# Fifty-two products of a constant tile with itself on TensorE's queue, from the launch to slot 4, in a two-layer cross-attention kernel

## The chip, the cores and the metric

The kernel runs on one core of one Trainium2 chip. A core has five engines with a queue each: TensorE (PE in the profile; its weight loads stand apart as PEld), VectorE (DVE), ScalarE (ACT), GpSimd (POOL) and SyncE (SP). The last of them, and in places ScalarE, issue DMA transfers. The metric is the device time of the whole program in microseconds (us), as the median of several executions.

## The reference

Two cross-attention layers follow each other on x of shape (16, 256, 320), with one context of shape (16, 256, 512) and 20 heads of 16. Of the context's 256 tokens, layer 0 takes the first 77 as text and the other 179 as image tokens; layer 1 takes the first 252 as text and the last 4 as image tokens. Layer 0, cut to what is computed:

```python
q = hidden_states @ Wq
k_text, v_text = text @ Wk, text @ Wv
probs = softmax(einsum('bhqd,bhkd->bhqk', q_h, k_h) * scale)
text_out = einsum('bhqk,bhkd->bhqd', probs, v_h)
scores = einsum('bhqd,bhkd->bhqk', q_h, ip_k_h) * scale
text_probs = softmax(einsum('bqc,bkc->bqk', q, k_text) * scale)
sem = einsum('bqc,bnc->bqn', einsum('bqk,bkc->bqc', text_probs, text), ip) * scale
ip_probs = softmax(scores + 0.5 * sem[:, None]) * spatial_mask[None, None, :, None]
out = (text_out + einsum('bhqk,bhkd->bhqd', ip_probs, ip_v_h)) @ Wout + bout + residual
```

Layer 1 has the same form, with a normalized semantic term for each head, and takes the output of layer 0 as its x. The products that the change adds belong to none of this: nothing reads them.

## The kernel before

**Slots.** Each layer is cut into NS = 80 slots; a slot is one of the 16 batch elements and four of its heads (five slots to an element). The loop at the end of the kernel runs the slots of layer 0 with `slot0(k)` and those of layer 1 with `slot1(k)`. What isn't the inner attention (projections of queries, keys and values, the semantic term, weights, the output projection) is cut into small steps, kept as `task` entries with due times in slots; `fill(now)` issues the steps that are due. So a step due at 1.85 comes late in slot 1. `RAMP` squeezes the due times of the first slots.

**A slot of layer 0.** `maxima0` turns the row maxima of the next slot's scores with two products against an identity (L752), copies them to `mt`, and four DMAs lay them as extra rows into `qs`. `score0` (L744) makes the scores of the slot after next in PSUM tile S for half of the queries at a time, and VectorE reduces them to maxima (L745, L746). `turned0` (L768) makes the scores of this slot turned over, in the two T tiles; ScalarE takes their exponential (L771) and GpSimd multiplies it with the semantic factor (L774). `attend0` multiplies the previous slot's probabilities with the values (L801, 24 instructions) into the one P tile, and `settle0` has VectorE read this tile: a transpose (L812), a reciprocal whose result is written back into the tile's first 16 columns (L815), a product there with the spatial mask (L816), and the product that reads these columns last (L818). `stacks` issues the DMAs that fill `qs` and `ks` for the slot LEAD = 4 ahead.

**PSUM tiles.** `kept` holds a ring of whole tiles for each of the tags T (two tiles) and P (one tile); `own(tag)` hands them out in turn. So `kept["P"][1]` is the one P tile that `attend0` and `settle0` use, and `kept["T"][1]` the first of the two T tiles.

**The beginning.** `begin()` is written out by hand: loads (`land`), the rounding of each operand into a high and a low part (`high` on ScalarE, `low` on VectorE or GpSimd), and the first keys, queries, semantic terms and values, up to the scores and maxima of slots 0 and 1. In it the order of all engines is the order of the code. In the loop only TensorE's order is that of the code; the orders of the other engines are planned from modelled times when the kernel is built, with some of them tied by `queued` and `anchor`. Tiles carry their dependencies: whoever writes a tile waits for those who still read that part of it.

**Number formats.** Most products are in fp32r (one instruction each). Products of plain F32 operands, as L801, L1064 and L468, take two instructions each, as the counts of the profile show (L468 is one product and stands there with two instructions).

Of the kernel before, what the change touches and what calls it, by code (L numbers as in the profile page):

```python
# [43 lines left out]
def RAMP(t):  # L44
    return t if t < -5 or t > 3 else (t + 5) * 0.375
PINNED = {getattr(mybir.EngineType, e) for e in ("PE",)}
BANKS = {"T": 2, "P": 1, "X": 3}


@with_exitstack  # L50
def xattn2(
# [27 lines left out]
    nc = tc.nc  # L79
    f = lambda ap: ap.bitcast(F32)  # L80
# [19 lines left out]
    def own(tag):  # L100

        n, *ring = kept[tag]
        kept[tag][0] += 1
        return ring[n % len(ring)]

    def scores(kept=False):

# [227 lines left out]
    def fields():  # L335

        ind0 = buf("nt", [128, 2, 8, 32], bufs=2, name="ind0").rearrange("p a f c -> p (a f c)")[:3, :S]
        dma(ind0[:2], ind0_d)
        dma(ind0[2:], ind0_d[:1])
        yield  # L340
        ind0r = buf("mt", [8, S], FR, name="ind0r")[:3]
        nc.scalar.copy(ind0r, ind0)
        yield
        for i in range(SIZES["NR"]):
            dma(ks[i][XROW + T0 : KS0, :, :T0], ind0r[:2, :T0].unsqueeze(1).to_broadcast([2, 4, T0]))
        for i in range(2):
            dma(buf("M", [TR, 2, S], FR, bufs=SIZES["M"])[T0:, 0], ind0r)
            dma(buf("tph", [TR, 2, S], FR, bufs=2)[T0:, 0], ind0r)
        yield
# [166 lines left out]
    def weights4(l):  # L516
        wo.append((yield from weights((wo0_d, wo1_d)[l], "wF", tmask[:, 4:5], (0.1, 0.3)[l], "rawc")))
# [186 lines left out]
    def stacks0(k, parts="KQTM"):  # L704
        b, g = divmod(k, NG)
        Q, K = QK[k] = qs[k % SIZES["NR"]], ks[k % SIZES["NR"]]
        for part in parts:
            if part == "K":
                anchor(dma(K[0:XROW], stack_rows(kd[0][b // 2][:, :, b % 2], g)))
            elif part == "Q":  # L710
                dma(Q[0:XROW], stack_rows(get("q0", b)[1], g))
            elif g < SIZES["NR"]:
                tph, mh = get("s0", b)[1::2] if part == "T" else (None, get("m0t", b))
                if part == "T":
                    dma(Q[XROW : XROW + TR], tph[:, 0:1].to_broadcast([TR, 4, S]))
                else:
                    dma(K[XROW : XROW + TR, :, T0:], mh[:, 0:1, T0:].to_broadcast([TR, 4, S - T0]))
# [19 lines left out]
    def score0(k, t):  # L737
        Q, K = QK[k]
        if t == 0:
            maxes[k] = buf("mn", [128, 2, 4, 2], FR, bufs=2)  # L740
        mn = maxes[k]
        sp = scores(True)
        for h in range(4):
            mm(sp[:, h], Q[: XROW + T0, h, t * 128 : (t + 1) * 128], K[: XROW + T0, h], start=True, stop=True)  # L744
        nc.vector.tensor_reduce(mn[:, t, :, 0], sp[:, :, :T0], axis=AX.X, op=ALU.max)  # L745
        anchor(nc.vector.tensor_reduce(mn[:, t, :, 1], sp[:, :, T0:], axis=AX.X, op=ALU.max))  # L746

    def maxima0(k, queue=nc.scalar):
        Q, mn = QK[k][0], maxes[k]
        mp = bank()  # L750
        for t in range(2):
            mm(mp[:8, t * 128 : (t + 1) * 128], mn[:, t].rearrange("p h a -> p (h a)"), ident_r, start=True, stop=True)  # L752
        mt = buf("mt", [8, S], FR)
        nc.scalar.copy(mt, mp[:8, :S])  # L754
        for h in range(4):
            issues[k] = queue.dma_start(f(Q[XROW + T0 : KS0, h]), f(mt[2 * h : 2 * h + 2]))
# [24 lines left out]
        settle0(b, g, pv)  # L781

    def slot0(k):
        if k > 0:
            yield lambda: maxima(k + 1)
        yield lambda: ahead(k + 2, 0)
        yield lambda: turned0(k, 0)
        yield 0.2
        if k > 0:
            yield lambda: attend0(k - 1)  # L790
        yield lambda: ahead(k + 2, 1)
        yield lambda: turned0(k, 1)
        yield lambda: stacks(k + LEAD)
        yield 0.6
        yield 1.0
# [292 lines left out]
    def task(key, times, make, *needs):  # L1088
        tasks[key] = [times, 0, make, needs, len(tasks)]
# [71 lines left out]
    task(("w2",), [71.6, 72, 72.2, 72.6, 73], weights2, ("q0", B - 1), ("w6",))  # L1161
    for i in range(2):
        task(("w3", i), [NS - 4 + 5 * i], weights3)
    task(("w4", 0), [2.6, 2.8, 3, 3.2], lambda: weights4(0), ("k0", 1))
    task(("w4", 1), spread(NS + 4, 0.33, 4), lambda: weights4(1), ("c0", B - 1))

# [4 lines left out]
    def ahead(k, t):  # L1171
        if k < NS:
            score0(k, t)
        else:
            both1(k - 2, t)

    def maxima(k):
        if k < 2 * NS:
            (maxima0 if k < NS else maxima1)(k)
# [3 lines left out]
    def begin():  # L1183
# [29 lines left out]

        named = lambda a: [(a, k) for k in range(4)]
        ind = fields()
        for k in range(4):
            land(("c", k), ("k", k))
        dma(x0, xT_d[0].rearrange("(k p) t -> p k t", p=128))
# [62 lines left out]
        get(*v0)  # L1281
        parts(v1)
        stacks0(2, "KQ")
        score0(0, 0)
        parts(q1)
        stacks0(2, "TM")
# [13 lines left out]
        parts(s1)  # L1300
        stacks0(3)
        parts(k1)
        score0(1, 1)
        parts(k1, k1)
        maxima0(1, nc.sync)
        resid0.append(load(xT_d[0], "xc"))
        dma(mk, mk_d)
# [97 lines left out]
```

## Time and profile before

| what | value |
|---|---|
| median of 3 runs | 1512.75 us (1506.99 to 1522.51) |
| span of the profiled execution | 1510.6 us |
| instructions in it | 36096 |
| PE busy | 1433.0 us (95%) |
| DVE busy | 1178.0 us (78%) |
| ACT busy | 883.7 us (59%) |
| POOL busy | 1213.3 us (80%) |
| mean granted TensorE clock | 0.976 |

The profiled execution's span is 2.15 us below the median and lies between the runs. The page's row PEclk gives the granted clock of TensorE in tenths of full speed for 40 slices of 37.8 us each. A row of the chain of waits reads: start, length, engine, tile, line. A row of the timeline reads: start, length from the first start to the last end, engine, line, operation, tiles, shape, count, and in brackets the idle time of the engine before it with what ended it. In the timeline successive matmuls overlap at their ends, so the distance from start to start is what a matmul costs the queue.

### The profile page before, as it was taken

To read this page: it belongs to the slowest core of one execution; us is meant where nothing else is said; L and a number is where in the kernel's file an instruction comes from. 1 tells how busy PE (TensorE), PEld (TensorE's weight loads), DVE (VectorE), ACT (ScalarE), POOL (GpSimd) and SP (SyncE) were. 2 spreads that over 40 slices of the span, in tenths; PEclk is the share of its full clock that TensorE was granted. 3 is DMA by queue.
4 is the path that set the end of the run, shared out by engine and by line. 5 is a ranking of instruction groups with operands and counts; after the bars stand their busy time and mean duration, and the time that the engine had idled before them with its cause. 6 is when DMAs were issued, how large, how long until landed. Compare 5 with 4: busy or idle time off the path is not lost.

```text
span 1510.6 us, 36096 instructions
## 1 busy us (share of the span) xinstructions
PE 1433.0 (95%) x12726; PEld 1161.7 (77%) x12726; DVE 1178.0 (78%) x2595; ACT 883.7 (59%) x1973; POOL 1213.3 (80%) x1302
## 2 busy tenths in 40 slices
PE   8789999999999999789999999999999999999996
PEld 7678888888878777576777777777777777777764
DVE  5457777777787788776887888878877887888885
ACT  5346565656555545455665666666666666666561
POOL 4259797979797978886698779887988798879785
PEclk9699999999999999898999999999999999999998
DMA  7867787778777867775434434443444344434311
GB/s 235 200 182 217 205 220 203 221 207 223 201 212 203 226 187 188 171 208 156 124 101 126 126 112 123 130 131 106 124 131 126 109 132 124 123 108 115 101 33 38
DMA packets 231018, 234.38 MB, mean 155 GB/s; under 512 B 39095, under 2 KB 200710, under 8 KB 230822
## 3 DMA queue, kind: packets, MB, share of 16 engines
q1 hardware_dynamic: 228630, 230.77, 55.2%
q8 instruction: 102, 1.67, 0.5%
q10 hardware_dynamic: 2208, 1.30, 0.4%
q14 instruction: 78, 0.64, 0.1%
HBM read 118.04 MB, written 77.10 MB: 129 GB/s over the span
## 4 chain that ended last, share of the span: by engine, by line
PE 76%; DMA 6%; DVE 6%; POOL 5%; issue 3%; ACT 2%; SPq 2%; ACTq 0%; POOLq 0%; DVEq 0%
PE X L939 15%; PE X L239 14%; PE P L801 7%; PE X L609 5%; PE S L744 5%; PE P L951 5%; PE P L961 4%; PE T L768 4%; PE S L897 3%; PE T L891 3%; PE X L612 2%; PE X L249 2%; POOL wt L930 2%; PE X L578 2%; PE X L1064 1%
## 5 line engine op out<-in xcount | busy, mean ns | idle before, releaser
L774 POOL TENSOR_TENSOR P<-P,rs 128x512 f32<-128x512 f32 x320 | 414.0, 1316 | 92.4 <-ACT P L771 91.5
L930 POOL TENSOR_TENSOR wt<-P,ctb 128x512 f32<-128x512 f32 x320 | 410.0, 1305 | 78.2 <-ACT ctb L929 78.2
L939 PE MATMUL X<-ctb,gm 128*128 128x512 f32 x1120 | 306.1, 402 | 5.6 <-DVE wt L940 5.5
L771 ACT ACTIVATE P<-T 128x512 f32<-128x512 f32 x320 | 175.9, 593 | 158.6 <-PE T L768 117.1
L940 DVE TENSOR_TENSOR wt<-X,wt 128x512 f32<-128x512 f32 x320 | 216.2, 680 | 42.7 <-PE X L939 37.3
L939 PEld LDWEIGHTS X<-ctb,gm 128*128 128x128 f32 x1120 | 195.9, 189 | 38.8 <-DVE wt L940 8.2
L911 ACT ACTIVATE P<-T 128x512 f32<-128x512 f32 x320 | 173.1, 593 | 77.9 <-PE T L891 74.6
L929 ACT ACTIVATE ctb<-P 128x512 fp32r<-128x512 f32 x320 | 187.0, 627 | 38.5 <-PE X L939 34.7
L899 DVE TENSOR_REDUCE mn<-S 128x4 fp32r<-128x1008 f32 x160 | 191.3, 1196 | 0.0
L746 DVE TENSOR_REDUCE mn<-S 128x4 fp32r<-128x716 f32 x160 | 142.3, 889 | 0.0
L801 PE MATMUL P<-P,vr 128*32 128x256 f32 x1920 | 127.2, 397 | 2.2 <-DVE tmp L818 2.0
L744 PE MATMUL S<-ks,qs 125*128 125x256 f32 x640 | 118.9, 310 | 7.9 <-DMA ks<-M 3.4
L744 PEld LDWEIGHTS S<-ks,qs 125*128 125x128 f32 x640 | 89.5, 197 | 43.2 <-issue 22.7
L1027 POOL TENSOR_TENSOR r<-u,rs 128x40 f32<-128x40 f32 (+2 forms) x17 | 108.7, 6394 | 3.7 <-DVE u L1024 3.7
L768 PE MATMUL T<-qs,ks 127*128 127x256 f32 x640 | 107.8, 292 | 0.6 <-DMA qs<-mt 0.5
L812 DVE STREAM_TRANSPOSE nt<-P 128x512 f32<-128x512 f32 x80 | 57.0, 712 | 52.9 <-PE P L801 52.4
L745 DVE TENSOR_REDUCE mn<-S 128x4 fp32r<-128x308 f32 x160 | 74.5, 466 | 28.4 <-PE S L744 28.2
L768 PEld LDWEIGHTS T<-qs,ks 127*128 127x128 f32 x640 | 92.2, 198 | 2.0 <-issue 0.9
L801 PEld LDWEIGHTS P<-P,vr 128*32 128x32 f32 x1920 | 57.1, 112 | 43.6 <-issue 5.5
L951 PE MATMUL P<-P,v1t 128*32 128x256 f32 x1280 | 86.5, 388 | 0.0
L609 PE MATMUL X<-ho,wF 128*128 128x256 f32 x512 | 76.0, 291 | 10.3 <-ACT mt L754 4.6
L961 PE MATMUL P<-wt,zone 128*32 128x256 f32 x1280 | 84.8, 379 | 0.3 <-DVE wt L940 0.3
(279 smaller groups left out, 2984.4 us busy)
## 6 DMA issues: line engine op xcount, KB each, us to landing
qd<-q SPq DMA_DIRECT2D x96, 256.0 KB
qs<-tph SPq DMA_DIRECT2D x64, 320.0 KB
rawc<-in_cT_dram SPq DMA_DIRECT2D x60, 256.0 KB
qs<-qd SPq DMA_DIRECT2D x80, 192.0 KB
ks<-kd SPq DMA_DIRECT2D x80, 192.0 KB
ks<-kd SPq DMA_DIRECT2D x160, 96.0 KB
qs<-qd SPq DMA_DIRECT2D x160, 96.0 KB
kd<-kst SPq DMA_DIRECT2D x57, 256.0 KB
```

The lines of the kernel that those rows point to most:

```text
L239: last = mm(out, lhs(a, k), rhs(b, k), start=i == 0, stop=i == len(terms) - 1)
L744: mm(sp[:, h], Q[: XROW + T0, h, t * 128 : (t + 1) * 128], K[: XROW + T0, h], start=True, stop=True)
L768: mm(st[p][:, j], K[:KS0, 2 * p + j, t * 128 : (t + 1) * 128], Q[:KS0, 2 * p + j], start=True, stop=True)
L771: exp = anchor(nc.scalar.activation(pt, st[p], AF.Exp, scale=SCALE))
L774: anchor(nc.gpsimd.tensor_mul(pt, pt, rs[:, t : t + 1].to_broadcast([128, 2, S])))
L801: mm(pv[32 * s : 32 * s + 32, o : o + S], v[:, vt, h : h + 32], P[k, s // 2][:, t, s % 2], start=vt < 2, stop=vt != 1,)
L899: anchor(nc.vector.tensor_reduce(maxes[k + 2][:, t], sp[:, :, :T1], axis=AX.X, op=ALU.max))
L911: anchor(nc.scalar.activation(P[k, u][:, t], st[u], AF.Exp, scale=SCALE))
L929: nc.scalar.activation(R[k, u][:, t], P[k, u][:, t], AF.Copy, scale=0.5)
L930: anchor(nc.gpsimd.tensor_sub(W[k, u][:, t], P[k, u][:, t], f(R[k, u][:, t])))
L939: mm(yp, gm[:, gb], R[k, u][:, kt], start=i == 0, stop=i == len(blocks[n]) - 1)
L940: nc.vector.tensor_mul(W[k, u][:, n], yp, W[k, u][:, n])
```

## The change

A helper `turning(n, src, bank)` puts n products of a 128x128 F32 tile with itself on TensorE's queue, written to the first 128 columns of the kept P tile, or T tile, which nothing reads afterwards. The source is the identity, but at the launch, where the identity isn't there yet, it is a tile that VectorE first fills with zeros (`hsn`, which the heads' results fill later). The calls:

- at the launch, before the first loads: 10, of zeros, to P
- in `begin`, before the first scores of slot 0: 7, to T
- in `begin`, before the second half of the scores of slot 1: 4, to P
- in `begin`, before the maxima of slot 1: 11, to P
- in slot 1, before `maxima(2)`: 2, and after it, before the scores of slot 3: 6, to P
- as a task of its own at 1.85, ahead of the query projection's step due at 1.875: 5, to P
- in slot 4, before `maxima(5)`: 7, to P

```diff
+PAUSES = {1: (2, 6), 4: (7, 0)}
...
+    def turning(n, src=None, bank="P"):
+
+        src = ident if src is None else src
+        for i in range(n):
+            mm(kept[bank][1][:, :128], src, src, start=True, stop=True)
...
     def slot0(k):
+        if k in PAUSES:
+            yield lambda: turning(PAUSES[k][0])
         if k > 0:
             yield lambda: maxima(k + 1)
+        if k in PAUSES:
+            yield lambda: turning(PAUSES[k][1])
         yield lambda: ahead(k + 2, 0)
...
+    task(("pause",), [1.85], lambda: iter([turning(5)]))
...
         ind = fields()
+        blank = hsn.rearrange("p a f r d -> p (a f r d)")
+        nc.vector.memset(blank, 0.0)
+        turning(10, blank[:, :128])
         for k in range(4):
             land(("c", k), ("k", k))
...
         stacks0(2, "KQ")
+        turning(7, bank="T")
         score0(0, 0)
...
         parts(k1)
+        turning(4)
         score0(1, 1)
         parts(k1, k1)
+        turning(11)
         maxima0(1, nc.sync)
```

## The prediction

> **What bounds the kernel now.** I read the page first, then the windows of TensorE's clock in stretches of 1 us, the timeline of TensorE up to 105 us, and the chain of waits over the same time.
>
> ```profile
> span 1510.6 us, 36096 instructions
> PEclk9699999999999999898999999999999999999998
> PE 76%; DMA 6%; DVE 6%; POOL 5%; issue 3%; ACT 2%; SPq 2%; ACTq 0%; POOLq 0%; DVEq 0%
> ```
>
> TensorE carries 76% of the chain that ends last, so what shortens its work at the right place shortens the kernel. The clock row says how much a better clock can be worth in all: only the second slice of 37.8 us is far from full, with 0.6 of the speed; the first slice stands at 9, and two dips come much later, where the change adds nothing. The windows show the second slice, and the dip near 100 us, more closely (columns: stretch, length, TensorE's busy time and instructions, granted clock, DMA share, GB/s):
>
> ```profile
> 40.00:41.00 1.00, 1.00 (x11) 0.94 1.03 269
> 47.00:48.00 1.00, 1.00 (x6) 0.64 1.09 379
> 54.00:55.00 1.00, 0.00 (x0) 0.77 1.08 378
> 71.00:72.00 1.00, 1.00 (x8) 0.70 0.06 16
> 98.00:99.00 1.00, 0.39 (x2) 0.96 0.93 223
> 105.00:106.00 1.00, 1.00 (x7) 0.63 0.00 0
> ```
>
> The clock has two values in these stretches, 1.00 and 0.50. A mean of 0.94 says that it fell at 40.88; in the same way it rose at 47.72, fell at 54.54, rose at 71.6, fell at 98.92 and rose at 105.74. The distances are 6.84, 6.82, 17.06, 27.32 and 6.82 us, which are 2, 2, 5, 8 and 2 times 3.41: the clock is set anew once in 3.41 us, by what went before. For the first 17 us the windows have no record and write 1.00; there I go by the price of the same products:
>
> ```profile
> 0.81 0.09 DVE L320 MEMSET zone<- 128x32 f32 x1 [0.81 <-PEq L1394]
> ...
> 5.08 4.11 PE L400 MATMUL X<-cta,wA 128*128 128x156 f32 x16 [5.08 <-ACT wA L1201]
> ...
> 14.71 1.97 PE L609 MATMUL T<-hq,wE 128*128 128x256 f32 x8
> ...
> 30.56 2.08 PE L609 MATMUL X<-hq,wE 128*128 128x256 f32 x16
> ...
> 39.73 0.71 PE L744 MATMUL S<-ks,qs 125*128 125x256 f32 x4 [1.82 <-DMA ks<-M]
> ...
> 52.83 0.74 PE L744 MATMUL S<-ks,qs 125*128 125x256 f32 x4 [0.90 <-DVE mn L746]
> ...
> 56.01 0.27 PE L752 MATMUL X<-ident_r,mn 128*8 128x128 f32 x1 [2.38 <-DVE mn L746]
> ...
> 61.28 0.27 PE L752 MATMUL X<-ident_r,mn 128*8 128x128 f32 x1 [0.42 <-DVE mn L746]
> ...
> 63.17 1.19 PE L744 MATMUL S<-ks,qs 125*128 125x256 f32 x4 [1.62 <-DMA ks<-M]
> ...
> 76.68 1.09 PE L609 MATMUL X<-hq,wE 128*128 128x256 f32 x7 [1.15 <-POOL hq L283]
> ...
> 88.52 0.77 PE L239 MATMUL X<-cta 128*77 128x192 f32 x6 [1.35 <-DVE q L167]
> ...
> 98.54 0.23 PE L752 MATMUL X<-ident_r,mn 128*8 128x128 f32 x1 [1.66 <-DVE mn L746]
> ```
>
> Eight products of L609 take 1.97 us at 14.71, sixteen take 2.08 us at 30.56: the first stretch of the kernel ran at half clock too, though TensorE had been busy since 5.08. The brackets are the pauses. The falls at 40.88, 54.54 and 98.92 each come at the end of a 3.41 us stretch in which TensorE stood still for some 1.6 to 1.9 us (1.82; 0.90 and the first part of 2.38; 1.66). After pauses of 1.15 and 1.35 us the clock stayed. So the pauses do lower the clock here, and the change puts its products exactly before the waits of these rows.
>
> What the half clock costs depends on the chain at that time:
>
> ```profile
> 15.80 3.68 DMA rs<-in_wvi_dram
> ...
> 58.09 4.95 DMA ks<-M
> ...
> 63.17 1.19 PE S L744 x4
> 64.37 0.85 PE T L768 x4
> 65.22 2.48 PE X L239 x12
> 67.70 2.72 PE P L801 x24
> 70.42 1.16 PE S L744 x4
> 71.57 0.56 PE T L768 x4
> ...
> 79.87 0.53 PE S L744 x4
> 80.40 0.48 PE T L768 x4
> ...
> 81.73 1.43 PE P L801 x24
> ```
>
> At 15.80 the chain is a load, and the row at 58.09 is the last of a long series of SyncE's issues and DMAs; a faster TensorE gains little or nothing there. From 63.17 to 72.13 it is TensorE alone, up to 71.6 at half clock. The same pieces at full clock, one slot later, have about half the price.
>
> **The change, part by part.** First the price of one product: two instructions of 128 columns, F32, each with a load of 128 columns of weights.
>
> ```profile
> 73.91 0.79 PE L239 MATMUL X<-cta,wA 128*128 128x156 f32 x6
> ...
> 527.47 0.43 PE L468 MATMUL X<-rawc 64*128 64x64 f32 x2
> ...
> 782.00 1.02 PE L1064 MATMUL X<-rs,rs 128*128 128x256 f32 x4
> ```
>
> The last row gives 0.26 us for an instruction of 256 columns, so 0.13 for half the columns at least; the first gives 0.13 for an instruction with a 128-column weight load; the middle one gives 0.43 for a whole small product that stands alone. The ends are 0.2 and 0.43; I take 0.24, nearest to sixteen in a row at 30.56 (0.13 each, with their tail), and 0.48 at half clock. All 52 are 12.5 us at full clock.
>
> *Launch, 10 products of zeros.* The fill of 768 columns is at most 24 times the 0.09 us of the 32-column row and lies in VectorE's idle start. The products then run from some point between 1 and 3 us for 4.8 us at half clock, and the first L400 begins 0.8 to 2.7 us late. That is hidden: the chain at that time is loads, up to 19.48. In return the clock may rise before 14.71, where eight products of L609 would take 1.04 instead of 1.97. Ends 0 and 0.93 us of gain, I take 0.45.
>
> *Before slot 0, 7, 4 and 11 products.* At full clock 1.68, 0.96 and 2.64 us against pauses of 1.82, 0.90 and 2.38. The overruns of 0.06 and 0.26 lie under the DMA that lands at 63.04. Cost 0; their use is that slot 0 and 1 find the full clock. If that cover were gone they would cost 0.3 us.
>
> *Slot 1, 2 and 6 products, and the 5 of the task.* 0.48, 1.44 and 1.20 us against 0.42, 1.62 and 1.15: 0.1 us over. The chain's pieces from 63.17 sum to 1.19 + 0.85 + 2.48 + 2.72 + 1.16 + 0.56 = 8.96 us. At full clock they are twice 0.53, twice 0.48, twice 0.79 and 1.43, together 5.03. The gain is at most 3.93, at least 0. What is late next is `hq` on GpSimd (76.68), behind the exponentials and GpSimd's products of the same slot, which have prices that TensorE's clock doesn't change but start earlier with it; I take 3.5.
>
> *Slot 4, 7 products.* Here a wait is added. They write the first 128 columns of the one P tile, which `settle0` still reads for slot 2:
>
> ```profile
> 92.86 1.50 PE L801 MATMUL P<-P,vr 128*32 128x256 f32 x24
> ...
> 100.17 0.41 DVE L818 TENSOR_TENSOR tmp<-nt,P 128x256 f32<-128x256 f32 x1
> ```
>
> and the chain of waits at this place:
>
> ```profile
> 101.69 2.72 PE P L801 x24
> 104.41 1.15 PE S L744 x4
> ```
>
> `attend0(2)` fills the tile at 92.86, VectorE's last reader of it, L818, ends at 100.58, and the next writer before was `attend0(3)` at 101.69, which lost nothing by it. The seven products stand at 96.88, where the pause of 1.66 us began, and must now wait until 100.58. Behind them on TensorE's queue are `maxima(5)`, L744 of slot 6, L768 of slot 4 and the L801 of 101.69; ScalarE, VectorE and GpSimd wait for these in turn. A pause of 3.7 us lowers the clock by the reading above, so the products take 7 x 0.48 = 3.4 us, up to 104.0; the maxima 0.3, L744 1.15 and L768 0.85 bring L801 to 106.3. L801, L744 and L768 then at full clock (1.43 + 0.53 + 0.48) end at 108.7. Before, L801 and L744 ended at 105.56, and with a last L768, priced like the 0.56 above, some 0.6 later at 106.2. Loss 2.5 us. With everything at full clock from 100.58 the same work ends at 106.0 (7 x 0.24, 0.3, 0.53, 0.48, 2.44) and loses nothing; with everything at half it loses 4.5.
>
> *Sum.* 1510.6 - 0.45 - 3.5 + 0.1 + 2.5 = 1509.2 us of span. The median stands 2.15 above this execution's span, so 1511.4; I say 1511.
>
> **The rivals.** *Both gain (1507).* VectorE's order in the loop is planned anew; with the products as waiters it may have L818 done before 97. For it: L818 is a short step that ran 5.8 us after L801's end, late through other work put ahead of it. Against: nothing in the change shortens that other work. Then slot 4 stays at full clock and gains 1.29 on L801 and 0.62 on L744: 1510.6 - 0.45 - 3.5 + 0.1 - 1.9 + 2.15 = 1507.0.
>
> *Slower: the clock is lost ahead of slot 1 all the same (1516.6).* Place: the wait for the maxima at 56.01. VectorE's work there hangs on loads, so when the earlier stretch at half clock (40.88 to 47.72) runs at full, TensorE arrives up to 3 us sooner and the wait grows. It decides if more than some 1.6 us of one stretch stay empty beyond the 11 products. Then the eight products of slot 1 cost 3.84 us against 2.04 of pauses, 1.8 over, and the 3.5 are not gained: 1510.6 - 0.45 + 1.8 + 2.5 + 2.15 = 1516.6. [...]
>
> *The products don't hold the clock (1519).* The falls would have another cause, or products of an identity would not count as work. Slot 1 then costs 1.8 over and slot 4 4.5: 1510.6 + 6.3 + 2.15 = 1519. Against it stand three falls, each after a pause. [...]
>
> *The plan of the other engines.* ScalarE, VectorE, GpSimd and SyncE are ordered from modelled times after slot 0, and 20 new products there move these.
>
> ```profile
> L771 ACT ACTIVATE P<-T 128x512 f32<-128x512 f32 x320 | 175.9, 593 | 158.6 <-PE T L768 117.1
> ```
>
> If one exponential in each of the 16 batch elements changed places with another piece of ScalarE's work on the chain, that is 16 x 0.59 = 9.5 us, either way: 1521 or 1502.
>
> **How the numbers follow.** Forecast 0.36, both gain 0.20, the clock lost ahead of slot 1 0.20, products that don't hold it 0.08, a worse plan 0.09, a better one 0.07. The likeliest case alone, with the ends of its terms, reaches from 1506 to 1516. The range of 1500 to 1521 takes in the cases up to the plan's centres and leaves out the outer parts of the two plans and the scatter of the runs, below 2 in 10. About 1% (15 us) is what a measurement of this kernel can tell from no change; all the half-clock stretches on the chain are worth less than that. Faster than 1497.6 needs a better plan and most of the gains (0.06), slower than 1527.9 a worse plan on top of a loss (0.06), and 0.88 is left for within 1%.
>
> **What would show it.** Right: the clock at full between 41 and 72 us, L801 of slot 0 near 1.5 us, L609 of the query projection about 3.5 us earlier than 76.68, and in slot 4 a product of `turning` with an idle time of 3 us or more ended by DVE L818. Wrong: half clock at the first L744 after 63 us (the third case), products at slot 4 that start at once (the second), first differences that begin only after slot 6 in the orders of ScalarE or VectorE (the plan), or a product that costs 0.4 us at full clock.

## The result, and the profile after

The changed kernel takes 1518.32 us in the median of 20 runs, the kernel before 1511.36 us in the median of 20 runs on the same chips. The ratio is 1.0041, with a 95% interval of 1.0022 to 1.0060: slower by 6.2 us, at least 3.3 and at most 9.1. Runs over 1.5% above the fastest of the same kernel count as slow: all 40 of these are fast, and for the kernels that are cut short below the medians stand with and without such runs. The profiled execution of the changed kernel has a span of 1520.1 us against 1510.6.

The page of the changed kernel first: span, granted clock in 40 slices, and the shares of the chain that ended last.

```profile
span 1520.1 us, 36309 instructions
...
PEclk9999999999999999898999999999999999999997
...
PE 73%; DVE 8%; DMA 6%; POOL 5%; issue 4%; ACT 3%; SPq 1%; ACTq 0%; DVEq 0%; POOLq 0%
```

The second slice of the clock row, 6 before, is 9 now: the part of the change that aims at the clock works. Between 26 and 110 us the granted clock is 0.50 for 6.8 us in this profile and for 30.7 in that of before. TensorE's share of the chain falls from 76% to 73%, VectorE's rises from 6% to 8%: the lost time is spent waiting for others.

The windows of the changed kernel (stretch, length, busy time and instructions of TensorE and then of the other engines, granted clock, DMA share, GB/s):

```profile
54.00:55.00 1.00, 1.00 (x11) 1.00 (x10) 1.00 (x3) 0.89 (x2) 0.00 (x0) 1.00 1.09 383
66.00:67.00 1.00, 1.00 (x8) 1.00 (x7) 0.86 (x2) 0.83 (x2) 0.15 (x1) 0.57 1.07 264
71.00:72.00 1.00, 1.00 (x10) 1.00 (x9) 1.00 (x3) 0.71 (x2) 0.04 (x1) 1.00 0.00 0
...
101.00:102.00 1.00, 1.00 (x7) 1.00 (x5) 0.00 (x0) 0.36 (x1) 0.00 (x0) 0.50 0.00 0
```

The fall at 54.54 is gone, the half clock of slot 1 is down to one stretch that begins near 66.1, and a new one lies at 101. The timeline of TensorE in the changed kernel shows the products (L111) themselves; the last column is the idle time before an instruction and what ended it:

```profile
1.72 3.90 PE L111 MATMUL P<-hsn 128*128 128x128 f32 x20 [1.72 <-DVE zone L327]
5.38 1.34 PE L407 MATMUL X<-cta,wA 128*128 128x156 f32 x8
...
38.22 1.72 PE L111 MATMUL T<-ident 128*128 128x128 f32 x14
...
60.52 1.55 PE L111 MATMUL P<-ident 128*128 128x128 f32 x12
64.82 0.71 PE L751 MATMUL S<-ks,qs 125*128 125x256 f32 x4 [2.75 <-DMA ks<-M]
...
75.66 1.49 PE L616 MATMUL X<-hq,wE 128*128 128x256 f32 x8
...
98.90 2.15 PE L111 MATMUL P<-ident 128*128 128x128 f32 x14 [2.71 <-DVE tmp L829]
...
103.00 1.81 PE L812 MATMUL P<-P,vr 128*32 128x256 f32 x24
```

The ten products of the launch begin at 1.72 and hold up the first L407 by only 0.30 us (5.38; 5.08 before). Seven products take 1.72 us, 0.246 each. At 98.90 stands the forecast wait: 2.71 us until VectorE's last reader of the P tile, and half clock behind it, from 100.26 to 103.68, within the 24 products of L812 at 103.00, which take 1.81 us. Yet this early part is not where the time went. The times at which the two profiled executions start the same TensorE instruction, read from their timelines:

```
                                   before   changed   difference
first scores of slot 3              63.2      64.8       +1.6
slot 5                             114.2     114.0       -0.2
layer 0                            260.0     260.3       +0.3
                                   366.5     373.8       +7.3
                                   554.7     565.3      +10.6
change of layers done              759.3     768.2       +8.9
layer 1, end                      1505.7    1515.0       +9.3
```

The kernels are even after slot 5. The changed one loses some 10 us between 260 and 555 us, where the change has no product, and both run alike through layer 1.

### The profile page after: what moved, and what is told of

The parts are those of the page before. It is cut to its first block, busy times and chain, and to the rows that moved or that the text cites. A ratio compares the mean times of both kernels' runs of the same rounds, so it can differ in the third digit from the quotient of the medians.

```text
span 1520.1 us, 36309 instructions
## 1 busy us (share of the span) xinstructions
PE 1442.1 (95%) x12830; PEld 1168.5 (77%) x12830; DVE 1181.3 (78%) x2596; ACT 884.5 (58%) x1973; POOL 1214.0 (80%) x1302
## 4 chain that ended last, share of the span: by engine, by line
PE 73%; DVE 8%; DMA 6%; POOL 5%; issue 4%; ACT 3%; SPq 1%; ACTq 0%; DVEq 0%; POOLq 0%
PE X L950 15%; PE X L246 14%; PE P L812 6%; PE X L616 5%; PE P L962 5%; PE S L751 5%; PE P L972 4%; PE T L775 4%; PE T L902 3%; PE S L908 3%; PE X L619 2%; PE X L256 2%; PE X L585 2%; PE X L1075 1%; POOL wt L941 1%
## 5 line engine op out<-in xcount | busy, mean ns | idle before, releaser
L812 PE MATMUL P<-P,vr 128*32 128x256 f32 x1920 | 128.5, 400 | 2.2 <-DVE tmp L829 1.9
L751 PE MATMUL S<-ks,qs 125*128 125x256 f32 x640 | 115.7, 304 | 4.7 <-DMA ks<-M 2.7
L752 DVE TENSOR_REDUCE mn<-S 128x4 fp32r<-128x308 f32 x160 | 74.7, 467 | 31.7 <-PE S L751 30.7
L812 PEld LDWEIGHTS P<-P,vr 128*32 128x32 f32 x1920 | 57.6, 114 | 44.9 <-issue 8.2
```

The lines of the kernel that those rows point to most:

```text
L812: mm(pv[32 * s : 32 * s + 32, o : o + S], v[:, vt, h : h + 32], P[k, s // 2][:, t, s % 2], start=vt < 2, stop=vt != 1,)
```

## The experiments

**One part alone.** The changed kernel without slot 4's products, and the kernel before with slot 4's products only (it gets `turning`, the call at the head of `slot0` and `PAUSES = {4: (7, 0)}`). The edit of the first:

```diff
-PAUSES = {1: (2, 6), 4: (7, 0)}
+PAUSES = {1: (2, 6)}
```

> The changed kernel without the seven products of slot 4 (the other 45 stay). Slot-4 theory: the loss comes from the seven products, which wait 2.7 us for VectorE, and from the order of VectorE and ScalarE that is planned anew around them; without them the time falls to that of the kernel before or below, a ratio of 0.997 to 1.001. Shared-step theory: the loss comes from one VectorE step of the query split (the one that takes 3.65 instead of 0.8 us at 289 us) that gets stuck beside GpSimd's products in some slots and executions; its odds do not hang on slot 4 alone, so the ratio stays at 1.002 to 1.006.

> The kernel before with only the seven products of slot 4. Slot-4 theory: slower, ratio 1.003 to 1.007. Shared-step theory: as the kernel before, 0.998 to 1.003, and its profile shows as many steps of more than 3 us as its time is above 1505, divided by some 3 us.

Without slot 4's products: 1516.12 us, ratio 1.0024 [0.9992, 1.0055]. With them alone: 1516.03, ratio 1.0034 [1.0008, 1.0061]. The interval of the first takes in no change at all, so its loss isn't shown; the second is clear of noise. Neither theory fits both: the first ratio lies where the shared-step theory put it, the second where the slot-4 theory did, and the second one's profile has no step of more than 3 us in the query split, where the shared-step theory asked for four or five. The windows of the first one's profile show the clock when slot 4's products are absent:

```profile
66.00:67.00 1.00, 1.00 (x9) 1.00 (x9) 1.00 (x3) 0.19 (x1) 1.00 (x2) 1.00 0.95 206
...
101.00:102.00 1.00, 1.00 (x11) 0.94 (x10) 0.00 (x0) 0.48 (x2) 1.00 (x2) 1.00 0.87 216
```

The clock stays full at 101 us. Its profiled execution was also the fastest of its 12 runs (1503.83 us), so its trace says little of the others.

**A step that is sometimes held.** One of the jumps after slot 5 stands at VectorE's last step of the query split, `hl[:, 2]` in `split`, beside GpSimd's four products of the exponentials. In the changed kernel's timeline (VectorE, GpSimd, TensorE):

```profile
289.03 3.65 DVE L291 SCALAR_TENSOR_TENSOR hq<-hq,tmask,xq 128x256 fp32r<-128x256 f32 x1
...
285.76 5.01 POOL L781 TENSOR_TENSOR P<-P,rs 128x512 f32<-128x512 f32 x4
290.74 1.25 POOL L290 TENSOR_TENSOR hq<-xq,hq 128x512 fp32r<-128x512 f32 x1
291.96 0.44 POOL L830 TENSOR_TENSOR hsn<-tmp 128x128 f32<-128x128 f32 x1
...
292.88 1.25 PE L246 MATMUL X<-cta,wB 128*128 128x360 f32 x6 [2.50 <-DVE sp L676]
```

and the same place before:

```profile
288.70 0.79 DVE L284 SCALAR_TENSOR_TENSOR hq<-hq,tmask,xq 128x256 fp32r<-128x256 f32 x1
...
285.45 5.20 POOL L774 TENSOR_TENSOR P<-P,rs 128x512 f32<-128x512 f32 x4
...
289.93 1.14 PE L239 MATMUL X<-cta,wB 128*128 128x360 f32 x6
```

Same neighbours, same offset of 3.3 us from GpSimd's first product, and the step takes 0.79 us in one and 3.65 in the other, until GpSimd's queue pauses (its last product ends at 292.40, the step at 292.68); TensorE stands still for 2.50 us behind it. That GpSimd's products hold the step is read from this end; what in them would do so is not shown, and the short step before runs beside such products too. Moving the step to GpSimd, as a subtraction on 64 rows, in both kernels:

```diff
-        order(nc.vector.scalar_tensor_tensor(hl[:, 2], f(hl[:, 2]), neg, src[:, 2], op0=ALU.mult, op1=ALU.add))
+        order(eng.tensor_sub(hl[64:, 2], src[64:, 2], f(hl[64:, 2])) if neg is None else nc.vector.scalar_tensor_tensor(hl[:, 2], f(hl[:, 2]), neg, src[:, 2], op0=ALU.mult, op1=ALU.add))
...
-        xs = split(x, tmask[:, 5:6], nc.gpsimd, "hq") if b else xs0.pop()
+        xs = split(x, None, nc.gpsimd, "hq") if b else xs0.pop()
```

> The kernel before, with that step of the query split of layer 0 (elements 1 to 15) moved from VectorE to GpSimd, as a subtraction on the 64 rows that need it. Shared-step theory: no step of more than 2 us is left in the query split, the time falls by the 3 to 10 us that the stuck steps cost (ratio 0.992 to 0.998) and the runs lie closer together. Slot-4 theory: nothing is gained, ratio 0.998 to 1.004, since GpSimd gets 0.7 us more in each element.

> The changed kernel with the same step on GpSimd. Shared-step theory: the same time as the kernel before with that step moved, within 0.002. Slot-4 theory: slower than that kernel by 0.003 to 0.007.

1554.59 and 1560.31 us, ratios 1.0276 [1.0233, 1.0319] and 1.0282 [1.0220, 1.0343]. The 0.7 us that one theory gave to GpSimd was an estimate; half of the 1.25 us of L290 above, which has twice the columns, would be 0.63. No step was held, but both kernels became some 40 us slower, for a reason that no run separates, where one theory expected a gain and the other no change. The pair tells nothing of the difference either: the two medians are 5.7 us apart, but the second one's six runs spread from 1548.1 to 1573.7 us, and without the two above 1.5% over its fastest its median is 1552.0, below that of the first.

**Where the time is lost: kernels cut short.** The loop ends after slot 5, the sums so far are stored, and the rest is left out:

```diff
-        for k in range(2 * NS + 2):
+        for k in range(6):
...
-        fill(999)
+        dma(out_d[0].rearrange("(k p) t -> p k t", p=128), hsn.rearrange("p a f r d -> p a (f r d)"))
```

> The kernel before cut off after slot 5 of layer 0 (the rest is left out, and the output is only the heads' results so far): some 125 to 135 us. It is the measure for the two cut kernels beside it. Early theory (the changed kernel loses its time in the stretch that holds the products): this one is 3 to 7 us faster than the changed kernel cut in the same place. Late theory (the loss comes between slots 9 and 47, where some steps get stuck beside GpSimd): this one is as fast as the changed kernel or up to 6 us slower.

> The changed kernel cut off after slot 5 in the same way. Early theory: 3 to 7 us slower than the kernel before cut there. Late theory: 0 to 6 us faster; from the one profiled execution (equal at 114 us) some 0 to 1 us.

> The changed kernel without the seven products of slot 4, cut off after slot 5. By its profile in full length and that of the changed kernel (13.9 against 12.1 + 13.3 - 7.5 = 17.9 us from the maxima of slot 5 to the first L239 after them), 3 to 5 us faster than the changed kernel cut there; 7 to 9 us faster than the kernel before cut there if that profile is typical, and nothing if the clock's falls differ from execution to execution.

124.92, 124.37 and 121.25 us. In these medians the change gains 3.7 us without slot 4's products, and these products take 3.1 of it back; how firm that is follows below. The same after slot 21 and after slot 63, with a second profile of each whole kernel beside them:

> The changed kernel once more, for a second profile of it. Late theory: its first 125 us are within 3 us of the first profile's, and the differences of the two profiles lie in single jumps of 1.5 to 4.3 us between 190 and 560 us, each at a step of more than 3 us on VectorE or at a fall of the clock.

> The kernel before, cut after slot 21 (the loop ends there and the sums so far are stored; all later work is left out). Yardstick for the next two. In the profile of before that stretch ends near 350 us, so both theories expect 345 to 360 us. Cut after slot 5, changed and unchanged kernels were 0.5 us apart and the one without slot 4's products was 3.1 us faster; here both differences are read again, 16 slots later.

> The changed kernel, cut after slot 21. Theory A (GpSimd's products hold VectorE's query-split step, and the changed kernel loses those draws more often from slot 6 on): the loss builds up slot by slot, so this is 2 to 4 us slower than the cut kernel before, and the profile shows more steps of that split above 3 us. Theory B (the loss comes only later, where the plan of the other engines differs near 549 us, or at the change of layers): still 0.5 us faster, within 1 us. Theory C (there is no loss of its own; the whole kernels differ by the draw of clock falls): the difference follows the time at half clock, 0.48 us for each us.

> The changed kernel without slot 4's seven products, cut after slot 21. Theory A: the 3.1 us it had gained by slot 5 have gone, so within 1.5 us of the cut kernel before. Theory B: still about 3 us faster. Theory C: faster by what its time at half clock is less, 0.48 us for each us.

> The kernel before once more, for a second profiled execution of it: the query-split steps on VectorE between 125 and 530 us, and the falls of the clock there. Theory A: none or one of these steps above 3 us, as in the first profile (one, at 437.69), while the two profiles of the changed kernel had two and two. If this one has two or more, the count does not tell the kernels apart and theory A has lost its ground.

> The kernel before, cut after slot 63 (all later work is left out). Yardstick for the next two; its two profiles reach that place near 520 to 540 us.

> The changed kernel, cut after slot 63. Loss in the steady slots of layer 0 (steps of TensorE that wait for VectorE or ScalarE, each with a fall of the clock behind it): 4 to 7 us slower than the cut kernel before, and the jumps are seen in its profile. Loss at the change of layers, 550 to 760 us: still 1 to 2 us slower, as after slot 21.

> The changed kernel without slot 4's seven products, cut after slot 63; every engine's order is that of the kernel before. Loss in the steady slots: its lead of 5.2 us after slot 21 is gone or turned, 0 to 4 us slower than the cut kernel before. Loss at the change of layers: still 4 to 6 us faster.

> The changed kernel without slot 4's products once more, whole, for a second profiled execution. If the loss is in the steady slots, TensorE reaches the first matrix products of slot 5 some 5 us before the kernel before does, and loses that again in jumps of 2 to 4 us between 250 and 550 us. If it is at the change of layers, the lead lasts to 550 us and is lost between 550 and 760 us. If this execution keeps its lead too (about 1503 us), neither is shown and the loss is one of rare draws.

Medians in us, with the difference from the kernel before in brackets (six runs each for the cut ones, five for the last of slot 63; standard errors of their means are 0.5 to 2.9 us). Below, the same without runs that lie over 1.5% above the fastest of their kernel, and the number of runs that is left:

```
                 before       changed           without slot 4's products
after slot 5     124.92       124.37 (-0.6)     121.25 (-3.7)
after slot 21    246.71       247.84 (+1.1)     241.46 (-5.3)
after slot 63    569.07       573.48 (+4.4)     567.17 (-1.9)
whole           1511.36      1518.32 (+7.0)    1516.12 (+3.6, from its ratio)

within 1.5% of the fastest
after slot 5     123.0 (2)    120.3 (1, -2.8)   120.6 (4, -2.5)
after slot 21    245.1 (3)    245.5 (3, +0.4)   241.3 (5, -3.8)
after slot 63    568.4 (3)    566.7 (2, -1.7)   567.2 (5, -1.3)
```

(The 0.48 us of theory C: over the 12 runs of the whole kernel without slot 4's products the span grows by 0.48 us for each us at half clock, worked out from the spans and mean clocks of the runs.)

The two halves of the table disagree on where the changed kernel loses its time, so the medians of the cut kernels don't settle it. (The cut after slot 21 was expected at 345 to 360 us and that after slot 63 at 520 to 540; both places were misjudged.) The profiles do better, since each has the start of every TensorE instruction. The instruction at 114.2 us in the kernel before starts there at 112.8 us in the mean of six profiles, at 112.4 in the changed kernel (six) and at 109.1 without slot 4's products (five), with standard errors of 0.5, 1.2 and 1.4: differences of -0.4 and -3.7 us, close to those of all runs. From there to the instruction at 554.7 us, three profiles of before (two whole, one cut after slot 63) take 440.6 to 443.7 us and three of the changed kernel 447.2 to 453.7: 8.2 us more in the mean, with a standard error of 2.2. So most of the loss arises between slot 6 and slot 63.

The two more whole runs took 1523.8 us (changed) and 1511.83 (before), the second whole run without slot 4's products 1510.85. The second profile of the changed kernel reaches slot 5 4.8 us ahead of the first, more than the 3 that were expected. The second one without slot 4's products reaches it 2.1 us ahead of the first profile of before, where 5 were expected, and loses 4.3 us at a held step near 139 us and 3.1 at a late load near 516.

A worse plan of the other engines is not the reason in this stretch. In the traces of the changed kernel VectorE, ScalarE and GpSimd run their work in the order of before from 107 to 549 us and ScalarE and SyncE issue their DMAs in the same order all along; only near 100 to 107 us and from 549 us on do the orders differ.

Held steps above 3 us among the five places near 139, 212, 289, 363 and 438 us: one in each of three executions of the kernel before, two in each of three of the changed one, one, one and three without slot 4's products, none with slot 4's alone. Each puts TensorE back by 2.7 to 4.3 us. At 289 us the step is held in all three of the changed kernel and in none of the seven others.

**Without the held step.** So the step itself was left out of both kernels, for all batches but the first of layer 0:

```diff
-order(nc.vector.scalar_tensor_tensor(hl[:, 2], f(hl[:, 2]), neg, src[:, 2], op0=ALU.mult, op1=ALU.add))
+if neg is not None:
+    order(nc.vector.scalar_tensor_tensor(hl[:, 2], f(hl[:, 2]), neg, src[:, 2], op0=ALU.mult, op1=ALU.add))
...
-xs = split(x, tmask[:, 5:6], nc.gpsimd, "hq") if b else xs0.pop()
+xs = split(x, None, nc.gpsimd, "hq") if b else xs0.pop()
```

> The kernel before without the query split's last step (the small part of rows 64 to 127 of the third block of x is left out for all batches but the first of layer 0), so VectorE has no step there that GpSimd's products can hold. Yardstick for the next one. If held steps cost about 4 us each and one execution of the kernel before has about one, it is some 4 us faster than before, about 1507 us, and its runs lie closer together; if the other engines' order is planned differently in these slots, its own time may lie elsewhere, and only the difference of the two counts.

> The changed kernel with the same step left out. Held-step theory: the extra loss of the changed kernel was made of these draws, so it is within 1.5 us of the run above, as it is after slot 5 (0.4 us). Rival (the loss lies elsewhere in layer 0, whatever the split does): still 4 to 5 us slower than the run above.

1505.63 us (ratio 0.9953 [0.9931, 0.9976]) and 1514.74 us (1.0006 [0.9981, 1.0032]): 9.1 us apart in the medians, 7.4 in the means with a standard error of 1.4. The theory that the held step alone carries the difference falls: without the step the gap is as large as with it. (Both kernels leave a part of the reference out; they serve for this comparison alone.)

**What the traces have in common.** Between 114 and 555 us twelve traces agree to 0.1 us over most of the way (155 to 207 us of the kernel before, for example, takes 52.0 us in all of them). They differ by jumps at a few places: those of the split, but also 206, 430 and 516 us, and there the changed kernel waits for loads. In its timeline (ScalarE and TensorE near 206 us, VectorE and TensorE near 521):

```profile
205.06 0.62 ACT L171 CAST ctb<-rawc 128x512 fp32r<-128x512 f32 x1
206.94 0.62 ACT L171 CAST ctb<-rawc 128x512 fp32r<-128x512 f32 x1 [1.27 <-DMA rawc<-in_cT_dram]
...
208.25 0.36 ACT L761 CAST mt<-X 8x256 fp32r<-8x256 f32 x1
...
208.67 0.86 PE L619 MATMUL X<-ho,wF 128*128 128x256 f32 x5 [0.85 <-ACT mt L761]
...
520.97 2.68 DVE L462 TENSOR_TENSOR rawc<-rawc 64x512 f32<-64x512 f32 x1 [1.34 <-DMA rawc<-in_cip_dram]
...
524.38 1.87 PE L246 MATMUL X<-cta,wB 128*128 128x360 f32 x5 [2.85 <-DVE sp L676]
```

and before:

```profile
205.38 1.29 ACT L164 CAST ctb<-rawc 128x512 fp32r<-128x512 f32 x2
...
207.35 0.36 ACT L754 CAST mt<-X 8x256 fp32r<-8x256 f32 x1
...
207.84 0.78 PE L612 MATMUL X<-ho,wF 128*128 128x256 f32 x5
...
514.88 1.16 DVE L455 TENSOR_TENSOR rawc<-rawc 64x512 f32<-64x512 f32 x1 [0.41 <-DMA rawc<-in_cip_dram]
517.65 1.25 PE L239 MATMUL X<-cta,wB 128*128 128x360 f32 x6 [1.29 <-DVE sp L669]
```

ScalarE's rounding of the context waits 1.27 us for the load, the copy of the maxima stands behind it on ScalarE's queue, and TensorE waits 0.85 us for that copy. SyncE issues these loads at the same distance from the work in both kernels; they land later. The view of the DMA queues in the second execution of the changed kernel, over the 5.09 us from the issue of that load to ScalarE's copy (first row: the busy tenths of 16 engines in 40 slices; below, packets, MB and share per queue):

```profile
DMA  4000000079625676999998632210101000059999
...
q1 hardware_dynamic: 569, 0.69, 45.2%
q8 instruction: 1, 0.02, 2.7%
q10 hardware_dynamic: 14, 0.01, 0.5%
```

and in the second execution of the kernel before, from the issue to the landing of the same load:

```profile
DMA  1010110000278246185467699999999898999797
...
q1 hardware_dynamic: 504, 0.62, 60.7%
q10 hardware_dynamic: 12, 0.01, 0.7%
```

In the first, the engines have almost nothing left after slice 25, and for some nine slices a remainder of 0 or 1 tenth goes on (one engine of 16 alone would make 0.06): 15 of the load's 16 landing signals have come by then, the last comes 2.0 us later. Queue 8 has one packet in this stretch, 0.02 MB of instructions in one piece, with 2.7% of 16 engines x 5.09 us, or 2.2 us. If a share of the load stood behind it on one engine, that share would come last in this way; the trace doesn't name the engine of a packet, so this is a guess. In the second there is no such packet, and no such tail. Over the whole kernel this queue reads, on both pages,

```profile
q8 instruction: 102, 1.67, 0.5%
```

16 KB each. In every one of the twelve traces one such packet comes, in the mean, for each 254 to 256 instructions that TensorE starts (12726 matrix instructions, as many weight loads and some that only wait or signal, before), so I take them for TensorE's own instruction stream. The change puts 104 more of each kind at its head, 210 in all, and in the mean of the 102 packets of the two first profiles the nth still comes at the same count (0.2 instructions off, single ones with a scatter of 36), so it meets other work. Counted alone, at 256 to a packet, it should stand 256 - 210 = 46 instructions, or 2.4 us at 13.3 us per packet, later beside the same work; at the three places of the table it stands 3.2 to 3.7 us later in the mean. The place of the packet, and the landing of the last of the load's 16 signals, both in us from the start of the issue, worked out from the traces' packets and signals (a dash: no packet within 4 us):

```
                              load near 203     load near 428     `cip` load near 515
                              packet  landed    packet  landed    packet  landed
before                         -1.3    2.9        0.2    3.1       -3.0    2.5
before, second                 -1.7    3.2       -1.3    3.2       -1.1    3.5
before, cut after slot 63      -1.7    3.0       -0.9    3.0       -2.3    2.5
before, without the step       -1.6    2.9       -1.1    3.0       -3.1    2.4
without slot 4                  2.2    3.0         -     3.1       0.3     2.8
without slot 4, second          3.1    3.5         -     3.1       1.5     3.7
without slot 4, cut after 63    1.9    3.0         -     3.0       0.6     3.1
changed                         3.5    4.0        3.4    4.1       1.1     3.7
changed, second                 1.2    5.0        3.5    4.3       0.5     3.0
changed, cut after slot 63      2.9    3.4        1.1    4.6       0.9     3.4
changed, without the step       1.1    4.7        3.3    3.9       0.6     3.4
```

The packet's place belongs to the kernel, but moves by up to 2.5 us between executions (3.5 and 1.2 at 203 us). All four executions of the changed kernel have it within 4 us behind the issue at all three places, none of the four of before has it there at the first or third, and one, harmlessly, at the second. The kernel before is not spared, only luckier: the context comes in two loads 2.3 us apart, the table has the second, and its packets meet the first. At 424.3 us, with the packet 2.5 us behind the issue, the last signal of that first load came 2.0 us behind the fifteenth; ScalarE waited 0.2 us for it and TensorE not at all.

Over all 241 loads of context in these eleven profiles and that of the kernel with slot 4's products alone, between 130 and 530 us, the last signal came more than 0.8 us behind the fifteenth in 18 of the 67 loads that had such a packet 0.5 to 3.6 us after the end of the issue, and in 3 of the 174 others. That the packet delays the load is read from this count. The order in time doesn't always bear it out: in four of the changed kernel's twelve cases the packet begins at 3.3 to 3.5 us, after the fifteenth signal (3.0 to 3.1 us), and the last signal comes before the packet's end. The kernel with slot 4's products alone, whose packets stand elsewhere again, has its worst case at another load (timeline, ScalarE and TensorE):

```profile
285.44 0.62 ACT L171 CAST ctb<-rawc 128x512 fp32r<-128x512 f32 x1 [3.22 <-DMA rawc<-in_cT_dram]
...
287.16 1.23 PE L619 MATMUL X<-ho,wF 128*128 128x256 f32 x4 [2.80 <-ACT mt L761]
```

How much of the loss is this? The table takes four pairs of profiles: the first profiles of the two whole kernels, their second ones, those of the kernels cut after slot 63, and those without the split's step. It gives what the changed kernel takes more than the kernel before between the same TensorE instructions, from 114 us on, in us (a stretch is named by its times in the first profile of the kernel before):

```
                               first    second   cut after   without
                               pair     pair     slot 63     the step
135-155   held step              0.0     +4.2       0.0        0.0
207-212   late context load     +0.5     +3.1       0.0       +1.2
286-296   held step             +2.8     +3.5      +4.3       -0.3
361-372   held step             +4.2      0.0       0.0        0.0
430-436   late context load     +0.6     +0.8      +1.1       +0.4
436-448   held step (before)    -2.7     -2.6       0.0        0.0
505-540   late `cip` load       +4.5     +0.9       0.0       +0.4
the rest of 114-555             +0.9      0.0      -1.6       +2.0
114-555                        +10.8     +9.9      +3.8       +3.7
555-759   change of layers      -1.6     +4.8        -        +2.4
759-1506  layer 1               +0.4     +0.6        -        -0.7
```

The places of late loads have 5.6 of the 10.8 us in the first pair, 4.8 of 9.9, 1.1 of 3.8 and 2.0 of 3.7 in the others; held steps have 4.3, 5.1 and 4.3 in the first three. The price of a jump is not the wait alone. Where the granted clock falls to 0.50 behind it, the half clock comes on top: the held step at 289 us costs 2.8 us in the first profile, where the clock stays, and 4.3 in the cut one; at 517 us TensorE waits 1.6 us longer and loses 4.5, with half clock from 523.5 to 530.3. There the load has 0.9 us of VectorE's delay, and its step on the load takes 2.68 us against 1.16, with GpSimd's products running in both profiles. The change of layers, where the plan of the other engines does differ, adds 4.8 and 2.4 us in two of three pairs and nothing in the first.

In the pair without the step TensorE's wait at the first late load shows in the changed kernel (timeline, ScalarE and TensorE):

```profile
203.64 0.62 ACT L171 CAST ctb<-rawc 128x512 fp32r<-128x512 f32 x1 [1.93 <-DMA rawc<-in_cT_dram]
...
205.36 0.86 PE L620 MATMUL X<-ho,wF 128*128 128x256 f32 x5 [1.51 <-ACT mt L762]
```

**What stays open.** No run shifted TensorE's instruction stream by itself, say with products at a place without a pause. That the added instructions move the packets follows from the counts; that a packet is what makes a load late, and that the loss would go with it, was not tried. Held steps and late loads share the loss about evenly in the profiles, and no run tells why the step at 289 us is held in the changed kernel alone. The medians of the pair without the step differ by 9.1 us, its profiled spans, 1502.1 and 1505.9, by 3.8, and its changed kernel was profiled in its fastest run (1507.67 us; seven of its twelve lie above 1514), so some 5 us of its other runs are not seen in any trace. The kernel without slot 4's products has no late load that costs TensorE time at 206 or 430 us; its three long profiles have up to three held steps and one late `cip` load, and its loss is not clear of noise. No kernel that computes the whole reference came out faster than the one before; the 1505.63 us belong to one that leaves out a step.

## Why the prediction was wrong

The forecast was 1511 us, a gain of 1.4 on the profiled execution's own sum; it came out 6.2 us slower, inside the range but the other way. By its own steps:

- *Price of one product, 0.24 us:* 1.72 us for seven, 0.246. Right.
- *Launch, gain 0.45 of 0 to 0.93, and before slot 0, cost 0 under the DMA:* the record of the granted clock starts, at full speed, at 4.6 to 7.9 us in the eleven profiles with these products and at 16.0 to 17.1 in the six without, so the products do their work. The time did not follow: the first scores of slot 3 start at 63.9 us in the mean of the eleven and at 62.7 in the six, 1.2 later with a standard error of 0.5. The DMA still ends the wait ahead of them (2.75 us in the profile shown), and why it lands later is not shown. These two terms were off by 1.7 us together.
- *Slot 1, gain 3.5 of 0 to 3.93, less 0.1:* from these scores to the query projection's L609 the kernel before takes 13.4 us and the changed one 10.4, six profiles each: 3.0. Right, as a mean; the profiled execution got 2.3, with one stretch at half clock left at 66.
- *Slot 4, an added wait for L818, loss 2.5 of 0 to 4.5:* the wait is there (2.71 us, ended by L829, the L818 of before) and the half clock behind it too. The products start at 98.90 and not 100.58 and run at full clock up to 100.26, so the loss is smaller: from the instruction at 95.5 us to that at 114.2 the kernel before takes 18.0 us and the changed one 19.4 in the mean of six profiles each, 1.4 more (0.5 in the execution shown). Without slot 4's products the stretch takes 15.9, and in four of five profiles there is no half clock in it. The mechanism is right and the size within the range.
- *Pauses lower the clock:* in the 3.41 us ahead of the fall at 100.26 TensorE stood still for 2.0 us, the end of the pause of 2.71. In the first profiles of the two whole kernels every distance between two changes of the clock is 3.41 us or a multiple of it. Divided into such stretches, they have 25 falls: ahead of 23 TensorE stood still for 1.7 us or more of the stretch, ahead of the other two for 0.95 and 1.37. After 815 stretches the clock stayed full, and none of these has more than 1.66. So the reading holds in these two profiles. Executions of one kernel differ: of six profiles of before, three have the half clock from about 40 to 48 us and three don't, and the next fall comes between 53.8 and 57.0.
- *The sum:* this is the step that failed. It ends at slot 4: "1510.6 - 0.45 - 3.5 + 0.1 + 2.5" carries all the rest of the kernel over unchanged, as if the products cost only their own time and the waits beside them. Up to slot 5 it is near the truth, a gain of 1.4 forecast and 0.4 measured (six profiles each, standard error 1.3). Behind slot 5 the first pair loses 10.8 us up to 555 us and three pairs 8.2 in the mean, at loads that land late (about half), at held steps of VectorE and at the clock's falls behind both. The products are also 104 matrix instructions and as many weight loads at the head of TensorE's instruction stream, and move its packets against those loads. That this is the cause of the late landing is likely from the count of the loads, but no run tried it; why the held steps moved stays open.
- *The rivals:* slot 4 at full clock (1507) did not come. The clock lost ahead of slot 1 (1516.6) has nearly the measured time by luck, for after slot 5 the kernels are even; in two of six profiles it came in part (11.2 and 12.8 us of slot 1 against 13.4). Products that don't hold the clock (1519) are refuted by the clock row. A worse plan of the other engines (1521) places the loss rightly in later slots; but between 107 and 549 us the changed kernel's orders are those of before.

## What to carry to other kernels

A change's price does not end where its instructions end: when instructions are added to a full engine's stream, compare the time at which that engine reaches the same instruction all along the two traces, and look at each jump, above all at loads whose consumer stands only a few tenths of a us behind their landing. Cutting the kernel short at a few places tells in which stretch a small difference arises, but only when the difference is larger than the scatter of the cut kernels' runs; here the start times in several profiles told more than the medians. A load that the critical engine's neighbours take up in order deserves a microsecond or two of slack, since the last of its 16 signals, when it comes late, holds all that is queued behind (0.85 to 2.80 us of TensorE's time in the rows above). And a wait can cost twice: the same held step cost 2.8 us with the clock full behind it and 4.3 where the clock fell.

## What the runs showed of the hardware

One 16 KB packet of queue 8 took 0.9 to 1.9 us in the first profiles of the two whole kernels and 2.2 us in the row of the changed kernel's second, and the last of a load's 16 signals came up to 2.7 us after the fifteenth with such a packet beside it. TensorE shows no stop at the packets themselves (155 to 207 us takes 52.0 us in twelve traces, whose packets stand at different places); a wait came by way of the late load, 2.80 us of TensorE's time in the worst case.

VectorE's last step of the query split (L284 before, L291 in the changed kernel) took 0.46 to 0.85 us in 54 of its 64 cases in these two first profiles, 0.96 to 1.63 in seven and 3.46 to 3.67 in three. GpSimd was busy all through 49 of the 54 short ones as well, so its work beside the step does not by itself make it long. A single product of GpSimd takes 1.25 us here and the step at 289.03 took 3.65, the length of nearly three of them, until GpSimd's queue paused; why it is held in some cases and not in others, no run shows.
